# A layer of adaptive norm, long convolution and low-rank product: tables on ScalarE's queue, six weight buffers, rows in pairs

## Chip, cores and metric

The kernel runs on one core of a Trainium2 chip. The metric is the device time of one execution in microseconds. Before the change three runs took 2176.75, 2179.15 and 2181.75 us; the median is 2179.15.

## What is computed

x has 4 batches of 1024 rows of 2048 numbers, all fp32. From a short vector c per batch the modulation makes six vectors of 2048 (sections 0 to 5, in this order):

```python
mod = (silu(c) @ wmod).reshape(4, 6, 1, -1)       # wmod: 2048 x 12288
sa, ca, ga, sb, cb, gb = (mod[:, i] for i in range(6))
ga, gb = (sign(g) * max(abs(g), 0.25) for g in (ga, gb))
h = layernorm(x) * (1 + ca) + sa
x = x + ga * (causal_conv(h, K) + D * h)          # along each row, 2048 taps
h = layernorm(x) * (1 + cb) + sb
out = x + gb * (h @ W.T + bias + low_rank(h))     # 16 adapters of rank 16
```

The impulse response K comes from a state space model of 64 complex states: sums over the states at 2048 frequencies (with the parameters Lambda, p, q, Ct, Vc, Bp and log_step, and tables of cosines and sines), and an inverse Fourier transform.

## The kernel before

The work stands in stages that overlap. A tile scheduler puts each engine's instructions in a fixed order from the order of the source, the dependencies and marked priorities; each engine then takes its own list strictly in turn, and waits at a semaphore where data or a buffer is missing. The DMA queues of SP, ScalarE (ACT) and GpSimd (POOL) are lists of the same kind. Transfers share eight semaphores for SP and ACT together, taken in rotation, so that a transfer can also wait for the one that last used its semaphore.

**Modulation.** A section is 16 rows of weights (`mod_load`, L306): each a tile wm of 128 x 2048 fp32, 1 MB, loaded by SP (L309). `mod_mm` (L312) then issues four matmuls of 512 columns side by side into one PSUM tile, modps, of which there is one buffer; the left operand sct is silu(c). `section` in `net` (L792) runs over the 16 rows. At its end ScalarE copies modps to mrow (L325), TensorE transposes it (mtp, L328) and VectorE writes the column (L332): ca from section 1, sa from section 0, then both are scaled (`fold_scale`, L361 to L373). All sections share the pool wmp of WM = 3 buffers.

**Impulse response.** `toeplitz` (L233) calls `s4` (L76) with high priority. `s4` loads parameters and tables with 16 transfers of GpSimd (L86 to L107), five of them twice, for the upper and the lower 64 partitions. VectorE makes 2/step from log_step (z, L112 to L124), coefficients (L130 to L147), and in four chunks of 512 frequencies the terms of the sums: TensorE spreads the tables (s4cs, L161), VectorE and ScalarE work on wi, wr and nu (L165 to L173), TensorE sums over the states (s4rp, L176). VectorE continues on s4R (L181 to L226), TensorE ends the transform (s4kp, L229). The result kk is scaled with a maximum over partitions by GpSimd, stored to DRAM (kd, L254) and read back as overlapping rows kb (L258), all on ACT's queue. The second half of `toeplitz`, taken after row KT = 6 of section 0, reverses kb's rows on TensorE (kbps, L262) and splits it into fp16 parts kh and kl (L278 to L283).

**The start** (`net`, L838): section 1, then the loads of x blocks 0 to 2 and the statistics of blocks 0 and 1 (`conv_load`, `stats` L494), then section 0.

**Phase 1** runs over 32 blocks of 128 rows. `conv_prep` normalizes a block (n, L511), transposes it (tp, L532), modulates it (t, L535) and splits it into fp16 parts hc and hs (L541 to L544); `conv_mm` (L564) is the convolution, 108 matmuls a block; `conv_post` stores x (x1d) and the transposed second norm (n2d, L622). The gate's section 2 runs beside blocks 0 and 1. From block R0 = 3 on a filler `rest` is stepped by the plan of each block: it alternates between `merges` (low-rank product added to W, L440 lps, and operands wcd stored, L469) and the rows of sections 4, 3 and 5, one row after every MR = 2 merge steps.

**Phase 2** multiplies by the merged weights in Winograd's form (`ffn_unit`, L701), in 16 units for each half of the columns.

Of the kernel before, what the change touches and what calls it, by code (L numbers as in the profile page):

```python
# [14 lines left out]
BF16 = mybir.dt.bfloat16  # L15
# [5 lines left out]
PSUM = bass.MemoryType.PSUM  # L21
# [3 lines left out]
P = 128  # L25
D = 2048          # length of a row: model width and sequence of the convolution
NB = 4            # batches
NC = D // P       # chunks of 128 in a row
HC = NC // 2
NU = 16           # units of 256 rows  # L30
LNMAX = 46.0      # no entry of a layer norm over 2048 exceeds sqrt(2047)
FP_TOP = 4096.0   # fp16 operands are scaled to at most twice this


class Net:
# [11 lines left out]
    # ---- scales: powers of two that bring the largest entry into [top, 2*top)  # L47
# [15 lines left out]
    # ---- 1/sqrt(var + eps)  # L63
    def rstd(self, pool, var, out, n, name, scale=1.0):
        # a step of Heron's method refines the root
        v = self.nc.vector
        ve = pool.tile([P, n], F32, tag=name + "_v", name=name + "_v")
        t = pool.tile([P, n], F32, tag=name + "_t", name=name + "_t")
        v.tensor_scalar(ve, var, 0.25 * scale, 0.25e-5, MUL, ADD)
        self.nc.scalar.activation(t, ve, AF.Sqrt)  # L70
        v.reciprocal(out, t)
        v.scalar_tensor_tensor(t, ve, out, t, MUL, ADD)
        v.reciprocal(out, t)

    # ---- impulse response of the state space model: PSUM [l1, l2], l = 16*l1 + l2
    def s4(self, pool):  # L76
# [9 lines left out]
        for h in range(2):  # L86
            hp = slice(64 * h, 64 * h + 64)
            nc.gpsimd.dma_start(out=vec[hp, 0, :], in_=io["Lambda_ri"])
            nc.gpsimd.dma_start(out=vec[hp, 1, :], in_=io["p_ri"])
            nc.gpsimd.dma_start(out=vec[hp, 2, :], in_=io["q_ri"])  # L90
            nc.gpsimd.dma_start(out=vec[hp, 3, :], in_=io["Ct_ri"].rearrange("o n c -> (o n) c"))
            nc.gpsimd.dma_start(out=vc[hp], in_=io["Vc_ri"])
        bp = T([P, 64], "s4bp")
        nc.gpsimd.dma_start(out=bp, in_=io["Bp"].rearrange("m o -> (m o)").partition_broadcast(P))
        ls = T([P, 1], "s4ls")
        nc.gpsimd.dma_start(out=ls, in_=io["log_step"].partition_broadcast(P))
        # cosines and sines in three bfloat16 parts, summed and broadcast by the tensor engine
        cs = T([3, 2, D], "s4cs", BF16)
        nc.gpsimd.dma_start(out=cs, in_=io["t_cs"])
# [3 lines left out]
        nc.gpsimd.dma_start(out=csk, in_=io["t_csk"])  # L103
        tw = T([P, 2, 16, 16], "s4tw")
        nc.gpsimd.dma_start(out=tw, in_=io["t_tw"])
        dft = T([P, 2, P], "s4dft")
        nc.gpsimd.dma_start(out=dft, in_=io["t_dft"])  # L107

        # 2/step = 2*exp(-log_step): range reduction, polynomial, exponent bits
# [16 lines left out]
        # B = Vc Bp  # L126
# [5 lines left out]
        # numerators conj(ct)B, conj(ct)p, conj(q)B, conj(q)p  # L132
# [15 lines left out]
        # 1/w, w = i (2/step) S - lambda C: real part in the first 64 rows, imaginary part below  # L148
# [67 lines left out]
        # inverse transform: over k2 with the table, over k1 on the tensor engine  # L216
# [15 lines left out]
    # ---- Toeplitz operand kb[s, j] = K[j - s], in two fp16 parts; D is added to K[0]  # L232
    def toeplitz(self, pool):  # L233
# [21 lines left out]
        # row s starts P - 1 - s earlier; the tensor engine puts the rows in the opposite order  # L255
# [8 lines left out]
        # for outputs in pairs of chunks: K at even chunks (for sums of two operands), and the  # L264
        # differences to the chunk before and after; two fp16 parts each
# [21 lines left out]
    # ---- silu(c), transposed: [k = 16 p + j, batch], the batches repeated over 32 columns  # L287
# [14 lines left out]
    # ---- one section of the modulation: PSUM rows 32 q + b hold columns 512 q ..  # L302
# [18 lines left out]
    def mod_column(self, pool, name, plus_one):  # L321
        """[d in chunk, chunk, batch] of the section in modps"""
        nc, v = self.nc, self.nc.vector
        row = pool.tile([P, 512], F32, tag="mg0", name="mrow")
        nc.scalar.copy(row, self.modps)  # L325
        ps = self.tps.tile([P, 4, P], F32, tag="t", name="mtp")
        for c in range(4):
            nc.tensor.transpose(ps[:, c, :], row[:, ds(P * c, P)], self.ident)  # L328
        col = self.const(name, [P, NC, NB])
        src = ps.rearrange("p c (q r) -> p q c r", r=32)[:, :, :, 0:NB]  # L330
        dst = col.rearrange("p (q c) b -> p q c b", c=4)
        v.tensor_scalar(dst, src, plus_one, None, ADD)  # L332
        return col

    def mod_gate(self, pool, name, bias=None):
        """the gate by rows, in DRAM; with bias also gate*bias"""
        nc, v = self.nc, self.nc.vector
        g = pool.tile([P, 512], F32, tag="mg0", name="mg0")
        v.tensor_copy(g, self.modps)
        m = pool.tile([P, 512], F32, tag="mg1", name="mg1")  # L340
        nc.scalar.activation(m, g, AF.Abs)
        v.tensor_scalar(m, m, 0.25, None, ALU.max)
        v.tensor_scalar(g, g, 0.0, 2.0, ALU.is_ge, MUL)
        v.scalar_tensor_tensor(g, g, 1.0, m, SUB, MUL)
        outs = [g]
        if bias is not None:
            bt = pool.tile([P, 512], F32, tag="mg2", name="mg2")
            for q in range(4):
                nc.sync.dma_start(out=bt[32 * q : 32 * q + 32], in_=bias[ds(512 * q, 512)].partition_broadcast(32))
            v.tensor_tensor(bt, bt, g, MUL)  # L350
            outs.append(bt)
        res = []
        for i, t in enumerate(outs):
            dr = self.dram.tile([NB, D], F32, tag=f"{name}{i}", name=f"{name}{i}")
            for q in range(4):
                nc.scalar.dma_start(out=dr[:, ds(512 * q, 512)], in_=t[32 * q : 32 * q + NB])
            res.append(dr)
        return g, res

    # ---- scales of the normalized, modulated rows, per batch; folded into the columns in place  # L360
# [15 lines left out]
    # ---- low-rank factors in two fp16 parts; w_e and the inverse scale of A go into B  # L376
    def prep_lora(self, pool, tmp):
# [9 lines left out]
        # no entry exceeds the norm of its row  # L387
# [32 lines left out]
    # ---- merged weights of d chunks c and c + 8; the seven right operands in DRAM  # L420
    def merge(self, pool, tmp, c):
# [22 lines left out]
        # no entry exceeds the norm of its row  # L444
# [44 lines left out]
    # ---- phase 1: layer norm, modulation, transposed operand of the convolution  # L489
# [29 lines left out]
    def conv_prep(self, pl, r, x, st, out):  # L519
# [4 lines left out]
        # fp16 parts of the chunks, and of the sums of an even chunk and the odd one after it  # L524
# [70 lines left out]
    def conv_late(self, x, y, sums):  # L595
        """gate and residual of a block whose convolution ran before the gate was there"""
        v = self.nc.vector
        for q in range(2):
            sl = ds(1024 * q, 1024)
            v.tensor_tensor(y[:, sl], y[:, sl], self.gat[:, sl], MUL)  # L600
            v.scalar_tensor_tensor(y[:, sl], y[:, sl], 1.0, x[:, sl], MUL, ADD, accum_out=sums[:, q : q + 1])

    # ---- the second layer norm, transposed
# [21 lines left out]
    def gate_tile(self, pool, b):  # L625
        """the gate of a batch with the scales of the convolution's operands taken off, in all rows"""
# [14 lines left out]
    # ---- phase 2: left operands of the seven products of a unit  # L641
# [48 lines left out]
    def ffn_unit(self, pl, u, q, lf, wc):  # L690
# [34 lines left out]
        # Winograd's form; P4 comes with the opposite sign  # L725
# [28 lines left out]
M0, MR = 0, 2  # L754
# [3 lines left out]
WM = 3  # L758
LEFT0 = 30
KT = 6  # L760
# [11 lines left out]
def net(ctx: ExitStack, tc: tile.TileContext, io):  # L772
# [19 lines left out]
    def section(sec):  # L792
        for q in range(16):
            if q == 0:
                k.mod_begin()
            k.mod_mm(k.mod_load(wmp, sec, q), q)
            yield
# [32 lines left out]
    toe = k.toeplitz(pool(st, "st", 1))  # L830
    with tc.high_priority():
        take(toe, 1)
# [3 lines left out]
    for sec in (1, 0):  # L836
        for i, _ in enumerate(section(sec)):
            take(mer, M0)  # L838
            if sec == 0 and i == KT:
                with tc.issue_after(k.last.ins):  # L840
                    take(toe, 1)
        if sec == 1:
            for r in range(3):
                xs[r] = k.conv_load(pl, r)
            for r in range(2):
                sts[r] = k.stats(pl, xs[r], "1")
    st.close()
    for name, bufs in (("h", 2), ("n", 2), ("t", 2), ("y", 2), ("g", 1), ("nt", 2)):
        pl[name] = pool(left, "p1" + name, bufs)
    def rest():  # L850
        mods = (x for sec in (4, 3, 5) for x in section(sec))
# [18 lines left out]
    def load_w(q, i):  # L870
        """the two halves of a right operand; two of them take the places of x"""
# [29 lines left out]
    sec = section(2)  # L901
# [3 lines left out]
    take(sec, 16)  # L905
# [76 lines left out]
def tables():  # L982
    """cosines and sines; they depend on the shapes alone"""
# [17 lines left out]
def layout(inputs):  # L1001
# [4 lines left out]
    # [chunk pair, row of the pair's operand, half of e, half of d, d]  # L1006
# [20 lines left out]
```

## Time and profile before

| what | us |
|---|---|
| median of three runs | 2179.15 |
| the profiled execution, first to last instruction | 2174.4 |
| what lies between that span and the median | 4.75 |
| TensorE busy | 2090.6 |
| VectorE busy | 1356.8 |
| ScalarE busy | 938.0 |
| first matmul of section 1 | 6.5 |
| first matmul of section 0 | 72.75 |
| last matmul of section 0 ends | 121.3 |
| mean clock granted to TensorE, share of full | 0.975 |

The profiled execution has no separate time of its own: its span of 2174.4 us is read beside the median of the runs. A line of a timeline gives start, duration, engine, source line, operation, what is written and read, count, and in brackets the engine's idle time ahead of it with what ended it. PE is TensorE, PEld its weight loads, DVE VectorE, ACT ScalarE, POOL GpSimd; a q behind a name is that engine's queue. A line of the windows gives the stretch, its length, the busy time and instruction count of PE, PEld, DVE, ACT and POOL, then TensorE's clock, the DMA engines' busy share and GB/s.

### The profile page before, as it was taken

The numbers are of one execution on the slowest core, as the hardware profiler recorded it, in microseconds if no ns is written. First come the engines' busy times: TensorE is split into PE (matmuls) and PEld (weight loads), VectorE is DVE, ScalarE is ACT, GpSimd is POOL, SyncE is SP. The second block draws the span as 40 slices with busy tenths as digits, with TensorE's granted clock in tenths as the row PEclk, the third lists the DMA queues.
The fourth block names the chain that finished last, engine by engine and source line by source line (L and its number), as shares of the span: only waits on it lengthen the run. The fifth ranks groups of instructions, "written<-read, shape, count | busy, mean of one in ns | idle before, by whom it ended". The sixth has DMA issues, their size and how long they took to land.

```text
span 2174.4 us, 28541 instructions
## 1 busy us (share of the span) xinstructions
PE 2090.6 (96%) x11084; PEld 1020.7 (47%) x11084; DVE 1356.8 (62%) x2293; ACT 938.0 (43%) x1795; POOL 11.7 (1%) x28
## 2 busy tenths in 40 slices
PE   4699999999999999999999999999999999999998
PEld 1234555555555555565444444444444444444443
DVE  5637898888989999974666666666533333333333
ACT  0046877767867778863353545454300000000000
POOL 1000000000000000000000000000000000000000
PEclk6589999999999999999999999999999999999999
DMA  7988687888788656747766666666785544544541
GB/s 273 368 325 307 232 315 271 300 313 299 278 307 300 219 204 232 257 136 294 264 223 232 222 219 221 232 223 225 285 332 192 174 164 164 175 165 165 172 157 68
DMA packets 207307, 516.62 MB, mean 238 GB/s; under 512 B 16112, under 2 KB 81665, under 8 KB 180289
## 3 DMA queue, kind: packets, MB, share of 16 engines
q1 hardware_dynamic: 206208, 513.11, 66.3%
q8 instruction: 87, 1.43, 0.3%
q10 hardware_dynamic: 388, 1.16, 0.1%
q0 software_dynamic: 576, 0.54, 0.1%
q14 instruction: 48, 0.39, 0.1%
HBM read 325.89 MB, written 188.85 MB: 237 GB/s over the span
## 4 chain that ended last, share of the span: by engine, by line
PE 64%; DVE 13%; ACT 8%; DMA 6%; issue 2%; SPq 1%; DVEq 0%; ACTq 0%
PE fZ L701 18%; PE fY L701 12%; PE fX L701 11%; PE ya L564 9%; PE yb L564 5%; PE lps L440 3%; PE modps L314 3%; DMA gt<-n2d 2%; DVE lf L662 2%; ACT gt L651 2%; PE tp L620 2%; DVE s L668 1%; ACT t L535 1%; ACT n L611 1%; PE tp L532 1%
## 5 line engine op out<-in xcount | busy, mean ns | idle before, releaser
L701 PEld LDWEIGHTS <-lf 128*128 128x128 f16 x5376 | 526.4, 98 | 642.0 <-issue 10.2
L701 PE MATMUL fZ<-w,lf 128*128 128x512 f16 x2304 | 514.8, 380 | 6.2 <-ACT p L709 6.1
L701 PE MATMUL fX<-w,lf 128*128 128x512 f16 x1536 | 342.6, 379 | 0.0
L701 PE MATMUL fY<-w,lf 128*128 128x512 f16 x1536 | 342.5, 379 | 0.0
L564 PEld LDWEIGHTS <-hc 128*128 128x128 f16 x2304 | 215.7, 98 | 187.9 <-issue 31.9
L717 DVE TENSOR_TENSOR xo<-xo,gb 128x1024 f32<-128x1024 f32 x64 | 78.3, 1224 | 204.6 <-DMA xo<-x1d 204.5
L535 ACT ACTIVATE t<-tp,sa,ca 128x128 f32<-128x128 f32 x512 | 200.1, 471 | 6.0 <-DVE sa L373 3.8
L651 ACT ACTIVATE gt<-gt,sb,cb 128x256 f32<-128x256 f32 x256 | 132.1, 594 | 148.2 <-DMA gt<-n2d 147.4
L564 PE MATMUL ya<-kh,hs 128*128 128x512 f16 (+3 forms) x768 | 192.9, 326 | 0.9 <-ACT hs L543 0.9
L564 PE MATMUL ya<-kh,hc 128*128 128x512 f16 (+3 forms) x768 | 192.7, 326 | 0.5 <-ACT qs L577 0.5
L564 PE MATMUL yb<-kh,hc 128*128 128x512 f16 (+3 forms) x768 | 192.5, 326 | 0.0
L314 PE MATMUL modps<-wm,sct 128*32 128x512 f32 x768 | 132.1, 728 | 27.9 <-DMA wm<-in_wmod 27.9
L564 PEld LDWEIGHTS <-hs 128*128 128x128 f16 x1152 | 107.5, 98 | 96.9 <-issue 15.9
L709 ACT COPY p<-fZ 128x512 f32<-128x512 f32 x64 | 37.3, 583 | 256.9 <-PE fZ L701 256.9
L709 ACT COPY p<-fX 128x512 f32<-128x512 f32 x32 | 18.5, 578 | 268.7 <-PE fX L701 255.7
L564 PE MATMUL ya<-kl,hc 128*128 128x512 f16 (+3 forms) x384 | 125.1, 326 | 0.0
L564 PE MATMUL ya<-kl,hs 128*128 128x512 f16 (+3 forms) x384 | 125.1, 326 | 0.0
L564 PE MATMUL yb<-kl,hc 128*128 128x512 f16 (+3 forms) x384 | 125.1, 326 | 0.0
L661 ACT CAST lf<-s 128x1024 f16<-128x1024 f32 x64 | 67.2, 1050 | 102.5 <-DVE s L668 75.8
L621 ACT COPY nt<-tp 128x512 f32<-128x512 f32 x128 | 74.8, 597 | 60.0 <-PE tp L620 40.9
L544 DVE TENSOR_TENSOR hc<-t,hc 128x512 f16<-128x512 f32 x128 | 87.3, 682 | 6.3 <-ACT hc L543 5.8
L723 DVE TENSOR_TENSOR xo<-xo,fin 128x512 f32<-128x512 f32 x128 | 88.2, 689 | 3.1
(247 smaller groups left out, 2234.3 us busy)
## 6 DMA issues: line engine op xcount, KB each, us to landing
wm<-in_wmod SPq DMA_DIRECT2D x96, 1024.0 KB
lfd<-lf SPq DMA_DIRECT2D x112, 512.0 KB
lf<-lfd SPq DMA_DIRECT2D x112, 512.0 KB
x<-in_x SPq DMA_DIRECT2D x32, 1024.0 KB
x1d<-y SPq DMA_DIRECT2D x32, 1024.0 KB
n2d<-nt SPq DMA_DIRECT2D x128, 256.0 KB
gt<-n2d SPq DMA_DIRECT2D x128, 256.0 KB
xo<-x1d SPq DMA_DIRECT2D x64, 512.0 KB
```

What stands on the lines that cost most here:

```text
L314: self.last = self.nc.tensor.matmul(self.modps[32 * g : 32 * g + 32, :], self.sct[:, j].rearrange("p r b -> p (r b)"), w[:, ds(512 * g, 512)],
L440: nc.tensor.matmul(ps, la[:, x, k, h], y[:, k, osl], start=(n == 0), stop=(n == 5))
L535: nc.scalar.activation(t[:, k], tp[:, k], AF.Identity, bias=self.sa[:, c, b : b + 1], scale=self.ca[:, c, b : b + 1],)
L544: v.tensor_tensor(lo[:, sl], src, hi[:, sl], SUB)
L564: nc.tensor.matmul(pf[:, o:512], h, self.kf[f][z][:, ds(k0, 512 - o)], start=first, stop=(i == last and (x, z) == (1, 0)), skip_group_chec ...
L621: nc.scalar.copy(nt, tp)
L651: nc.scalar.activation(t[:, c], t[:, c], AF.Identity, bias=self.sb[:, c, b : b + 1], scale=self.cb[:, c, b : b + 1],)
L661: nc.scalar.copy(hl[:, :, 0, :], s)
L701: nc.tensor.matmul(ps[name], lf[i][:, k, x, :], wc[i][k // 4][:, k % 4, y, :], start=(first and n == 0), stop=(n == 3 * HC - 1), skip_grou ...
L709: nc.scalar.copy(t, ps[name])
L717: v.tensor_tensor(x, x, self.gbias, ADD)
L723: v.tensor_tensor(xs[r][:, h], xs[r][:, h], t, ADD)
```

## The change

Three things change; comments in the source go too, which moves line numbers only.

```diff
 # s4: loads of parameters and tables
-        for h in range(2):
-            hp = slice(64 * h, 64 * h + 64)
-            nc.gpsimd.dma_start(out=vec[hp, 0, :], in_=io["Lambda_ri"])
...
-            nc.gpsimd.dma_start(out=vc[hp], in_=io["Vc_ri"])
+        def twice(x, n):
+            return bass.AP(tensor=x.tensor, offset=x.offset, ap=[[0, 2], [n, 64], [1, n]])
+        ls = T([P, 1], "s4ls")
+        nc.scalar.dma_start(out=ls, in_=io["log_step"].partition_broadcast(P))
+        nc.scalar.dma_start(out=vec[:, 0, :], in_=twice(io["Lambda_ri"], 2))
+        cs = T([3, 2, D], "s4cs", BF16)
+        nc.scalar.dma_start(out=cs, in_=io["t_cs"])
+        nc.scalar.dma_start(out=vc, in_=twice(io["Vc_ri"], 128))
         bp = T([P, 64], "s4bp")
-        nc.gpsimd.dma_start(out=bp, in_=io["Bp"].rearrange("m o -> (m o)").partition_broadcast(P))
...
+        nc.scalar.dma_start(out=bp, in_=io["Bp"].rearrange("m o -> (m o)").partition_broadcast(P))
+        for i, n in ((1, "p_ri"), (2, "q_ri"), (3, "Ct_ri")):
+            nc.scalar.dma_start(out=vec[:, i, :], in_=twice(io[n], 2))
...
-        nc.gpsimd.dma_start(out=csk, in_=io["t_csk"])
+        nc.scalar.dma_start(out=csk, in_=io["t_csk"])
...
 # net
-M0, MR = 0, 2
+MR = 4
-WM = 3
+WM, WMS = 3, 3
+X0 = (7, 11)
-KT = 6
+KT = 8
...
-    def section(sec):
-        for q in range(16):
-            if q == 0:
-                k.mod_begin()
-            k.mod_mm(k.mod_load(wmp, sec, q), q)
+    def section(sec, n, pools):
+        k.mod_begin()
+        for q in range(0, 16, n):
+            ws = [k.mod_load(pools[j % len(pools)], sec, j) for j in range(q, q + n)]
+            for j, w in enumerate(ws):
+                k.mod_mm(w, q + j)
             yield
...
+    wms = pool(st, "wms", WMS)
...
     for sec in (1, 0):
-        for i, _ in enumerate(section(sec)):
-            take(mer, M0)
+        for i, _ in enumerate(section(sec, 1, (wms, wmp))):
             if sec == 0 and i == KT:
                 with tc.issue_after(k.last.ins):
                     take(toe, 1)
-        if sec == 1:
-            for r in range(3):
+            if sec == 0 and i in X0:
+                r = X0.index(i)
                 xs[r] = k.conv_load(pl, r)
-            for r in range(2):
                 sts[r] = k.stats(pl, xs[r], "1")
+    xs[2] = k.conv_load(pl, 2)
     st.close()
...
-        mods = (x for sec in (4, 3, 5) for x in section(sec))
+        mods = (x for sec in (4, 3, 5) for x in section(sec, 2, (wmp,)))
...
-    sec = section(2)
+    sec = section(2, 2, (wmp,))
...
-    take(sec, 16)
+    take(sec, 8)
```

The 16 transfers of GpSimd become 11 on ACT's queue, in a new order: log_step, Lambda, the cosine table, Vc, Bp, then p, q and Ct, the table csk, tw and dft; those that were made twice now read their source twice with a step of 0. Sections 1 and 0 take their rows alternately from wms and wmp, six buffers together; wms lies in the stack `st`, which is closed after section 0, and the pools of phase 1 take its place. Blocks 0 and 1 of x are loaded after rows 7 and 11 of section 0, block 2 after its last row. Sections 2, 4, 3 and 5 load two rows and then issue both rows' matmuls; the filler takes such a pair after every four merge steps. In the built order of TensorE, the first five s4cs matmuls now stand ahead of section 1's first row.

More of the change, by code (lines that the diff above doesn't have):

```diff
@@ L85, in s4 @@
         vc = T([P, 64, 2], "s4vc")
-        for h in range(2):
-            hp = slice(64 * h, 64 * h + 64)
[L88 to L91, printed above, removed]
-            nc.gpsimd.dma_start(out=vc[hp], in_=io["Vc_ri"])
-        bp = T([P, 64], "s4bp")
-        nc.gpsimd.dma_start(out=bp, in_=io["Bp"].rearrange("m o -> (m o)").partition_broadcast(P))
[L95 to L99, printed above, removed]
+        def twice(x, n):
[6 more added lines that the diff above has]
+        nc.scalar.dma_start(out=vc, in_=twice(io["Vc_ri"], 128))
+        bp = T([P, 64], "s4bp")
+        nc.scalar.dma_start(out=bp, in_=io["Bp"].rearrange("m o -> (m o)").partition_broadcast(P))
+        for i, n in ((1, "p_ri"), (2, "q_ri"), (3, "Ct_ri")):
+            nc.scalar.dma_start(out=vec[:, i, :], in_=twice(io[n], 2))
         one = T([3, P], "s4one", BF16)
@@ L102, in s4 @@
         csk = T([P, 2, 16], "s4csk")
-        nc.gpsimd.dma_start(out=csk, in_=io["t_csk"])
+        nc.scalar.dma_start(out=csk, in_=io["t_csk"])
         tw = T([P, 2, 16, 16], "s4tw")
-        nc.gpsimd.dma_start(out=tw, in_=io["t_tw"])
+        nc.scalar.dma_start(out=tw, in_=io["t_tw"])
         dft = T([P, 2, P], "s4dft")
-        nc.gpsimd.dma_start(out=dft, in_=io["t_dft"])
+        nc.scalar.dma_start(out=dft, in_=io["t_dft"])
         z = T([P, 4], "s4z")
```

## Prediction

> **What bounds the kernel now.** I read the page's busy line and slices first, then the timelines of TensorE, GpSimd and ScalarE over the first 125 us, then the windows and waits.
>
> ```profile
> PE 2090.6 (96%) x11084; PEld 1020.7 (47%) x11084; DVE 1356.8 (62%) x2293; ACT 938.0 (43%) x1795; POOL 11.7 (1%) x28
> PE   4699999999999999999999999999999999999998
> PEclk6589999999999999999999999999999999999999
> ```
>
> TensorE bounds it from the third slice (54 us each) on. In the first two it is 40 and 60% busy at a clock of 0.5 to 0.6. So the prize lies in the first 121 us: the two modulation sections, 32 rows of 1 MB.
>
> ```profile
> 18.55 1.93 PE L314 MATMUL modps<-wm,sct 128*32 128x512 f32 x8 [0.64 <-DMA wm<-in_wmod]
> 29.84 2.29 PE L161 MATMUL s4cs<-s4cs,s4one 3*128 3x512 bf16 x5 [9.35 <-DMA s4cs<-in_t_cs]
> ...
> 61.10 1.88 PE L176 MATMUL s4rp<-s4coef,s4nu 128*128 128x8 f32 x8 [1.43 <-DVE s4nu L173]
> 62.90 3.64 PE L314 MATMUL modps<-wm,sct 128*32 128x512 f32 x16
> ...
> 72.75 1.93 PE L314 MATMUL modps<-wm,sct 128*32 128x512 f32 x8 [1.91 <-DMA wm<-in_wmod]
> 75.16 1.94 PE L314 MATMUL modps<-wm,sct 128*32 128x512 f32 x8 [0.47 <-DMA wm<-in_wmod]
> ...
> 119.34 1.93 PE L314 MATMUL modps<-wm,sct 128*32 128x512 f32 x8 [0.56 <-DMA wm<-in_wmod]
> ```
>
> TensorE stands 9.35 us for the cosine table, then takes rows two at a time between steps of VectorE's chain. A row costs 1.85 us at this clock (3.64 for two); rows arrive 2.48 us apart when transfers run freely (75.16 - 72.75 and the next). With three buffers the transfers stop whenever TensorE does:
>
> ```profile
> 20.00:30.00 10.00, 0.65 (x5) 0.20 (x2) 3.33 (x29) 0.00 (x0) 3.42 (x7) 0.50 0.74 245
> 30.00:66.00 36.00, 28.35 (x128) 9.98 (x126) 33.53 (x70) 4.82 (x8) 0.00 (x0) 0.55 0.77 282
> 66.00:72.70 6.70, 2.70 (x12) 1.65 (x8) 5.55 (x18) 1.87 (x2) 0.00 (x0) 0.50 1.00 419
> ```
>
> The last columns are clock, DMA share and GB/s: 245 and 282 against 419. Why the table is late:
>
> ```profile
> 1.25 0.85 POOL L88 DMA_DIRECT2D s4vec<-in_Lambda_ri  x1 [0.32 <-issue]
> 13.60 0.28 POOL L237 TENSOR_SCALAR_AFFINE_SELECT rev<-rev 128x128 f32<-128x128 f32 x1 [11.50 <-issue]
> ...
> 21.77 0.57 POOL L99 DMA_DIRECT2D s4cs<-in_t_cs  x1
> ```
>
> The reader is to see that the table is not slow to move but late to be asked for: GpSimd stands 11.5 us ahead of its mask, then issues a transfer each 0.55 us, and the cosine table is the thirteenth; it lands 8.0 us after issue (the page's list of issues).
>
> **Part 1, tables by ACT's queue.** Removed: 16 GpSimd transfers and that delay. Added: 11 issues on ScalarE at 0.23 to 0.53 us (its two early ones). The mask still waits to 13.6, but its first users now (identity: section 1's transpose, past 55) hide that; were they the first matmuls, it would cost 11 us. In the built order a transfer waits for the one that last used its semaphore: rows 2 and 3 on SP wait for the cosine table and Bp, p for log_step, Ct for Lambda, csk for row 0 (landed at 6.5), and ScalarE's tanh is queued behind csk. VectorE's sct follows that tanh among the products with Ct, so row 0's matmul starts near 12.5, not 6.51. That is hidden: six rows can be on their way, the last landing at 4 + 6 x 2.5 = 19, and row 6's buffer is free at 14.4; with three buffers it would stop the transfers from 11.5 on. Landing after issue: 2.1 us on empty queues (mc, issued 0.72, used 2.85) to 4.9 us under load (kd<-kk, 77.99 to 82.95).
>
> Two rules of the Trainium skill speak against this part, both in "DMA: Bandwidth & Descriptors". By "Issuing engines are not separate DMA queues", changing the issuer saves only issue time: by it 16 x 0.55 less 11 x 0.4, an estimated 4 us. The trace decides: the 11.5 us stand before the issues, the queues are not the limit. "Rules for kernel authors" says that a leading zero-stride broadcast of c copies keeps a transfer on c engines; the doubled loads have c = 2. Five of the eleven are confined so, which no run here shows; I price it at nothing to 5 us on Ct, taking 2, since they are small. So Ct lands at about 10 (7 to 14): issue 5, landing 3, confinement 2.
>
> The chain then, by VectorE's rows of before: coefficients, tanh products and sct 3.5, to 13.5; first combine (33.62) to s4R (63.01) 29.4, to 43; s4R to the last sum 6.3 without the column step, and its matmul 0.8, to 50. kk to its scaled form took 7.1 us, of which some 5 were statistics of x, now later: 2, to 52. Kd, then kb: 5.0, to 57. In the new order section 1's mrow stands on ScalarE behind both issues:
>
> ```profile
> 66.61 0.59 ACT L325 COPY mrow<-modps 128x512 f32<-128x512 f32 x1 [10.55 <-PE modps L314]
> ...
> 77.99 0.35 ACTq L254 DMA_DIRECT2D kd<-kk  x1
> 82.95 0.35 ACTq L258 DMA_DIRECT2D kb<-kd  x1
> ```
>
> Queued behind mrow are the square roots; waiting for it are the transpose and, since modps has one buffer, all of section 0. Rows 13 to 15 follow kp and end at 50 + 3 x 1.85 = 55.6, so the new wait costs 1.4 us. mrow 0.6 and transpose 1.1: row 16 starts at 58.7, where before it was 72.75.
>
> **Part 2, six buffers and later x.** Without stops, 32 rows, two x, kb and 0.5 MB of tables are 35.5 x 2.5 = 89 us from about 4: 93. Stops left: row 22 needs row 16's buffer (60.5), by when kb and row 21 are still moving (to 62); I take 2 us. TensorE: 58.7 + 16 x 1.85 + kbps 6.6 = 95 without a pause; I take 97 with row waits, the page's code fetches and the first bytes. Before, the last row ended at 121.3: gain 24.3. The kbps block, which cost a stop of 5 us (99.6 to 105.5), is now bridged by buffers. Extra space costs no work. The pools opened after st.close() wait for row 30, two rows ahead of their first use: nothing, 2 us if they are late.
>
> x0 lands before row 24, x1 before row 28, x2 after row 31. x2's four statistics (0.62 each) now stand among the steps that scale ca and sa; three lie on the path to the first activation: 1.9 us lost. Section 2's first row comes behind x2, 5 us after row 31, while TensorE needs 4.5 us to reach it: 0.5 at most, within my rounding. The kb splits and x1's normalization end near 97.5, beside the sa step; hidden, but if kbps slips, they slip on.
>
> **Part 3, row pairs, MR 4.** The 64 row and merge matmuls move, none is added. A pair holds TensorE 2.0 us instead of 1.0 twice. The fill gets shorter: in the built order the last merge product stands at convolution matmul 2052, formerly 2376, the first at 360 in both: 15.7 blocks of 108 instead of 18.7. Is VectorE the bound then? It is busy for 445 of 500 us (windows, 300 to 800), 0.89, that is 25.4 us of a block's 28.5. Its merge steps are 131 of 450 us (groups, 250 to 700), 8.3 a block; times 18.7 / 15.7 they are 9.9, so 27.0. TensorE's share, 48 rows of 1.0 and 384 products of 0.216 (twelve took 2.59), 131 us, goes from 7.0 to 8.3 a block, 29.8 in all. 27.0 / 29.8 = 0.91: not yet. SP is the other risk (waits of SP, then of whom, us, times, longest; 200 to 1010):
>
> ```profile
> SPq L622 <- ACT nt L621: 288.0, 83, 17.9
> SPq L309 <- PE modps L314: 78.0, 17, 14.6
> ```
>
> SP stands 78 us behind row buffers already; behind such a load stand the stores of n2d, x1d and wcd and the loads of x. Yet TensorE's own waits there are some 20 us in all, none for a row. No trace shows pairs: between 3 us won (fewer changes of work) and 10 lost (half as many waits again); I take 1.4 lost, near the row for single ones, since the built order loads a pair's rows well ahead of its matmuls.
>
> Sum: 24.3 - 1.9 - 1.4 = 21. The span 2174.4 becomes 2153.4; the profiled times stand 4.75 below the median 2179.15 (work around the span), so 2158.
>
> **Rivals.** (a) Larger, 12%: no stop and TensorE at a higher clock (a run of three rows took 2.78 us at 99.62); section 0 ends at 93, 2179 - 27 = 2152. (b) Smaller, 20%: the doubled loads land late (Ct at 20), all behind them shifts by 10 us, mrow too, and section 0 ends at 107: 2168. For it: the semaphore chain through row 0 and ScalarE's order; against: ACT's queue is empty and the loads are under 64 KB. (c) It does not do what it says, 5%: the early gain is lost again where VectorE is near its limit (780 to 930, where it is 91 to 100% busy and TensorE 93%); some 2 us remain: 2177. (d) Slower, 8%: the pair's second load holds SP till the pair before has passed TensorE, stores of wcd behind it stop ScalarE's and VectorE's two-buffer steps, and TensorE's transposes wait. Price: 24 pairs at 1.1 us = 26, against a gain of 24.3 - 1.9 = 22.4: 2183. It decides from 0.93 us a pair. For it: n2d's 288 us of waits show how much SP stands; against: no matmul of modps waited after 200 us.
>
> **How the numbers follow.** My case, 55%, spans 2153 to 2165. With most of (a) and (b), 2148 to 2172 leaves two in ten out. Faster: 0.55 + 0.12 + 0.20 = 0.87; within 0.2% (4.4 us, about what this measurement can tell from no change): (c), 0.05; slower: (d), 0.08.
>
> **What would show it.** Right: s4cs before 8 us, section 0's first row near 59, its last near 97 (121), DMA above 350 GB/s from 20 to 95, convolutions about 22 us earlier throughout, TensorE's waits in the fill still near 20 us. Wrong: VectorE waiting past 12 us for s4vec, mrow after 62, rows of section 0 waiting for landings, or waits of tp and modps after 200 us grown by over 10 us.

## The result and the profile after

The changed kernel takes 2184.77 us (median of 13 runs, 2180.71 to 2190.86) beside 2179.15 us for the one before (13 runs, 2176.75 to 2184.43). The ratio is 1.0024, with an interval of 1.0015 to 1.0034: some 5 us slower. The forecast was 2158 and its range ended at 2172.

The profiled execution of after has a span of 2185.9 us and a time of its own of 2187.76, 3 us above its median. In all later executions the time is 1.7 to 2.1 us longer than the span (1.86 here), so the profiled one of before took some 2176.3, 3 us below its median. The spans therefore show 11.5 us where the medians show 5.6. Sizes are taken below from ratios and medians, places from the traces; a difference of few us between the later parts of two traces is not read.

The page's busy line and slices of after:

```profile
PE 2084.6 (95%) x11084; PEld 1026.0 (47%) x11084; DVE 1355.3 (62%) x2293; ACT 939.6 (43%) x1795; POOL 2.7 (0%) x12
...
PE   4699999999999999999999999999999999999998
...
PEclk8689999999999999999999999999999999999999
```

TensorE's slices tell the two kernels apart only by the clock of the first two (8 and 6 tenths, where 6 and 5 stood). The start has to be read row by row. TensorE's timeline of after:

```profile
13.02 2.29 PE L162 MATMUL s4cs<-s4cs,s4one 3*128 3x512 bf16 x5 [13.02 <-DVE s4zi L123]
23.87 5.33 PE L315 MATMUL modps<-wm,sct 128*32 128x512 f32 x24 [8.57 <-DVE s4t L142]
...
61.62 0.61 PE L230 MATMUL s4kp<-s4zz,s4dft 128*128 128x16 f32 x2 [0.97 <-DVE s4zz L227]
...
70.44 1.08 PE L329 MATMUL mtp<-ident,mrow 128*128 128x128 f32 x4 [3.33 <-ACT mrow L326]
71.45 5.45 PE L315 MATMUL modps<-wm,sct 128*32 128x512 f32 x40
...
110.50 1.93 PE L315 MATMUL modps<-wm,sct 128*32 128x512 f32 x8 [0.56 <-DMA wm<-in_wmod]
```

The first matmul runs at 13.02, where before row 0 ran at 6.51; row 0 now starts at 23.87. Section 0 starts at 71.45, only 1.3 us earlier than before, and ends at 112.4 instead of 121.3. The head start is 8.9 us, not 24.3. ACT's queue shows what was issued when:

```profile
1.22 1.12 ACTq L92 DMA_DIRECT2D s4vec<-in_Lambda_ri  x1
2.37 0.29 ACTq L95 DMA_DIRECT2D s4cs<-in_t_cs  x1
...
3.26 6.28 ACTq L98 DMA_DIRECT2D s4bp<-in_Bp  x1
...
12.92 1.27 ACTq L100 DMA_DIRECT2D s4vec<-in_Ct_ri  x1
```

VectorE's first use of Lambda and of Ct:

```profile
12.79 0.17 DVE L151 TENSOR_SCALAR s4nl<-s4vec 128x2 f32<-128x2 f32 x1 [7.88 <-DMA s4vec<-in_Lambda_ri]
...
22.39 0.16 DVE L140 TENSOR_TENSOR s4t<-s4vec,s4bq 128x1 f32<-128x1 f32 x1 [5.03 <-DMA s4vec<-in_Ct_ri]
```

Lambda, 1 KB, was issued at 1.22, and VectorE could use it only at 12.8, after 11.6 us. The cosine table was issued early and came just behind, at 13.0. Bp's issue took 6.28 us of the queue, and Ct was issued at 12.92 and used at 22.4. The waits of SP's queue from 0 to 115 us (who waited for what: us in total, times, longest) show the damage:

```profile
SPq L310 <- PE modps L315: 52.9, 21, 6.8
...
SPq L310 <- DMA s4cs<-in_t_cs: 10.8, 1, 10.8
SPq L310 <- DMA s4vec<-in_Ct_ri: 7.5, 1, 7.5
```

The loads of rows 2 and 4 stood for the cosine table and for Ct, 18.3 us together, because they take over the semaphores of those transfers. So four of the six buffers stood empty until 13.0 (row 2's load was issued at 12.99). In the windows from 10 to 15 us of after and then of before, the last column is GB/s:

```profile
10.00:15.00 5.00, 1.98 (x5) 0.54 (x4) 1.94 (x12) 0.00 (x0) 0.54 (x2) 1.00 0.54 63
```

```profile
10.00:15.00 5.00, 1.65 (x14) 0.16 (x8) 0.00 (x0) 0.00 (x0) 1.39 (x3) 0.86 0.99 333
```

The second loss lies in the fill. The last merge product ends at 716.8 us instead of 774.4, as the built order said, but between 300 and 700 us TensorE is busy for 9.7 us less (before, then after; the first busy time is PE's, the third VectorE's):

```profile
300.00:700.00 400.00, 395.88 (x2512) 214.53 (x2510) 352.55 (x680) 285.53 (x578) 0.00 (x0) 1.00 0.86 301
```

```profile
300.00:700.00 400.00, 386.19 (x2427) 209.68 (x2425) 347.17 (x664) 282.77 (x555) 0.00 (x0) 1.00 0.87 309
```

VectorE is not busier than before, so its busy share does not explain this. TensorE's longest group of waits from 250 to 1000 us is for ScalarE's t, ahead of the transposes; before and after:

```profile
PE tp L532 <- ACT t L535: 5.4, 8, 1.4
```

```profile
PE tp L533 <- ACT t L536: 13.4, 13, 1.7
```

A third loss lies between the two. Block 3 of the convolution took 47.8 us, where before it took 37.6. Some of that is filler moved into it; but TensorE stood idle for 6.7 us in it instead of 2.3, at a lower clock (block 3 of after, then of before; the third figure from the end is the clock):

```profile
208.80:256.60 47.80, 41.15 (x220) 20.94 (x221) 36.64 (x78) 34.94 (x70) 0.40 (x1) 0.93 0.74 263
```

```profile
216.20:253.80 37.60, 35.28 (x201) 19.59 (x202) 33.00 (x69) 30.86 (x62) 0.40 (x1) 0.95 0.78 274
```

### The profile page after: what moved, and what is told of

The parts are those of the page before. It is cut to its first block, busy times and chain, and to the rows that moved or that the text cites. A ratio compares the mean times of both kernels' runs of the same rounds, so it can differ in the third digit from the quotient of the medians.

```text
span 2185.9 us, 28516 instructions
## 1 busy us (share of the span) xinstructions
PE 2084.6 (95%) x11084; PEld 1026.0 (47%) x11084; DVE 1355.3 (62%) x2293; ACT 939.6 (43%) x1795; POOL 2.7 (0%) x12
## 4 chain that ended last, share of the span: by engine, by line
PE 55%; issue 24%; DVE 10%; DMA 6%; ACT 5%; SPq 1%; ACTq 1%; POOL 0%; DVEq 0%; POOLq 0%
PE fZ L702 20%; PE fY L702 13%; PE fX L702 13%; PE ya L565 4%; PE yb L565 2%; DVE lf L663 2%; DMA gt<-n2d 2%; ACT t L536 1%; DMA wm<-in_wmod 1%; DVE s L669 1%; PE modps L315 1%; ACT gt L652 1%; DMA xo<-x1d 1%; ACT n L612 1%; PE tp L621 1%
## 5 line engine op out<-in xcount | busy, mean ns | idle before, releaser
L565 PEld LDWEIGHTS <-hs 128*128 128x128 f16 x1152 | 108.0, 98 | 92.7 <-issue 12.7
L315 PE MATMUL modps<-wm,sct 128*32 128x512 f32 x768 | 122.3, 693 | 28.7 <-DMA wm<-in_wmod 20.1
L533 PE MATMUL tp<-ident,n 128*128 128x128 f32 x512 | 80.5, 282 | 18.0 <-ACT t L536 16.0
L495 DVE BATCH_NORM_STATS2 st<-x 128x6 f32<-128x512 f32 x128 | 83.0, 680 | 18.4 <-DMA x<-in_x 18.4
```

Of the source, the lines that this page charges most:

```text
L315: self.last = self.nc.tensor.matmul(self.modps[32 * g : 32 * g + 32, :], self.sct[:, j].rearrange("p r b -> p (r b)"), w[:, ds(512 * g, 512)],
L495: v.bn_stats(st[:, q], x[:, ds(512 * q, 512)])
L533: nc.tensor.transpose(tp[:, k], n[:, ds(P * (c0 + k), P)], self.ident)
L565: nc.tensor.matmul(pf[:, o:512], h, self.kf[f][z][:, ds(k0, 512 - o)], start=first, stop=(i == last and (x, z) == (1, 0)), skip_group_chec ...
```

## The experiments

Two questions followed. Why did the tables land late, and what does each part of the change cost by itself? The first four kernels take them up. They ran beside a median of 2182.44 us for before (55 runs).

**Tables alone.** The kernel before with the 11 transfers of ACT's queue, three buffers and single rows.

```diff
-            nc.gpsimd.dma_start(out=vec[hp, 0, :], in_=io["Lambda_ri"])
+        nc.scalar.dma_start(out=vec[:, 0, :], in_=twice(io["Lambda_ri"], 2))
...
```

> The kernel before with the 11 table transfers on ScalarE's queue, nothing else. In the profile of after, Lambda landed at 12.8 us and the last of Ct near 16.8, the response's last matmul (s4kp) ended at 62.2 instead of 70.8, and TensorE stood 8.6 us for sct. Theory (doubled loads confined to few engines are late, but still earlier than GpSimd's): s4kp about 8 us earlier, with three buffers a part of it is lost again; section 0 ends 3 to 8 us earlier, 2171 to 2176. Rival (the new place on ScalarE's queue is itself the harm: sct and mrow stand behind transfers): section 0 ends no earlier, 2179 to 2184.

Measured 2180.45, ratio 0.9987 (0.9978 to 0.9996): 1 to 5 us gained. Section 0 ended at 118.6, 2.7 us earlier, a little under the theory's 3 to 8. The start is as late as in after: Lambda used at 12.7, row 0 at 20.2. The tables come earlier than from GpSimd, but the first rows pay for it.

**Buffers alone.** GpSimd's tables, single rows, six buffers, x after rows 7 and 11 and after row 15, the second half of `toeplitz` after row 8.

```diff
-        for i, _ in enumerate(section(sec)):
+        for i, _ in enumerate(section(sec, 1, (wms, wmp))):
```

> The kernel before with six buffers for sections 1 and 0, x loaded after rows 7, 11 and 15 of section 0 and KT 8; tables stay on GpSimd, later rows single. Theory: the buffers bridge TensorE's standing for the tables and the kbps block (some 5 us), x2's late statistics cost 2: section 0 ends 4 to 10 us earlier, 2170 to 2177, and nothing is lost in the blocks from 3 on. Rival (the new start, with x2's statistics and pools that wait for wms, disturbs the blocks that follow): block 31 at least 8 us later than section 0's end would give, 2180 to 2190.

Measured 2179.38, ratio 0.9979 (0.9971 to 0.9988). Section 0 ended at 112.5, as early as in the whole change, with the tables as late as before: the buffers alone give 8.8 us. Some 4.6 of them reach the end (2.6 to 6.3 by the interval).

**Pairs alone.** The start of before, sections 2 to 5 by pairs.

```diff
-MR = 2
+MR = 4
...
-        mods = (x for sec in (4, 3, 5) for x in section(sec))
+        mods = (x for sec in (4, 3, 5) for x in section(sec, 2, (wmp,)))
```

> The kernel before with later sections by row pairs and a pair after every four merge steps, nothing else. In the profile of after, block 3 stood 4 us ahead of before and block 31 10 us behind. Theory (the loss of some 15 us is made by the pairs and the denser fill): start as before, block 31 later by 10 to 18 us, 2189 to 2197. Rival (the loss comes out of the changed start): 2177 to 2182.

Measured 2195.10, ratio 1.0049 (1.0032 to 1.0065): 7 to 14 us lost, where the prediction had 1.4. This part alone turns the change from a gain into a loss.

**Halved loads.** The whole change, but each doubled load is two loads of 64 partitions, on the same queue; 16 transfers in place of 11.

```diff
-        def twice(x, n):
...
+        def both(out, x):
+            for h in range(2):
+                nc.scalar.dma_start(out=out[64 * h : 64 * h + 64], in_=x)
...
-        nc.scalar.dma_start(out=vec[:, 0, :], in_=twice(io["Lambda_ri"], 2))
+        both(vec[:, 0, :], io["Lambda_ri"])
...
```

> The changed kernel with each of the five doubled loads split in two loads of 64 partitions, still on ScalarE's queue, so 16 transfers; the leading step of 0 is gone. Theory (confinement to few engines makes Lambda, the cosine table behind it and Ct late): Lambda lands by 6 us, SP's row 2 goes out by 7 instead of 12.9, sct by 16 instead of 23, section 0 ends 5 to 10 us earlier than 112.4, 2174 to 2180. Rival (lateness comes from the semaphores in rotation and ScalarE's order, which more transfers make worse): section 0 ends at 112 or later, 2184 to 2188.

Measured 2181.48, ratio 0.9997 (0.9988 to 1.0007), with the pairs still in it: some 6 us faster than the whole change by the ratios, whose intervals lie apart. TensorE's timeline, VectorE's first use of Lambda and one window:

```profile
15.71 4.74 PE L315 MATMUL modps<-wm,sct 128*32 128x512 f32 x24
...
101.40 1.94 PE L315 MATMUL modps<-wm,sct 128*32 128x512 f32 x8 [0.56 <-DMA wm<-in_wmod]
```

```profile
9.89 0.17 DVE L151 TENSOR_SCALAR s4nl<-s4vec 128x2 f32<-128x2 f32 x1 [4.93 <-DMA s4vec<-in_Lambda_ri]
```

```profile
10.00:15.00 5.00, 2.29 (x5) 0.67 (x5) 4.32 (x18) 1.54 (x2) 0.54 (x2) 1.00 0.91 307
```

Row 0 starts 8.2 us earlier than in after, section 0 ends at 103.3 instead of 112.4, and the DMA engines move 307 GB/s where they moved 63. So the form of the loads, with what hangs on it, was the fault. The theory was too hopeful in two places: Lambda was used at 9.9 instead of 6, and row 2's load went out at 9.81 instead of 7. By the Trainium skill ("DMA: Bandwidth & Descriptors", "Rules for kernel authors") a leading broadcast of two copies holds a transfer to at most two of the sixteen engines, and the recovery agrees with that. So do the trace's records of single DMA packets: the first 128 packets of 8 bytes on ACT's queue, Lambda's by size and order, moved from 6.0 to 12.1 us in after and from 5.2 to 9.0 here, though issued at the same time beside the same two rows. The edit also shifts which semaphore each load takes over, and SP still stood 7.6 us for Lambda; so beyond these 3 us the run does not say how much of the 8.2 is due to either.

The next four ask whether gains and costs add, and what it is about pairs that costs. They ran beside a median of before of 2182.30 us (27 runs).

**The change without its pairs.**

```diff
-MR = 4
+MR = 2
...
-        mods = (x for sec in (4, 3, 5) for x in section(sec, 2, (wmp,)))
+        mods = (x for sec in (4, 3, 5) for x in section(sec, 1, (wmp,)))
```

> The change without its pairs: MR 2 and single rows in sections 2 to 5, the tables on ACT's queue and six buffers kept. Theory (the pairs cost some 13 us by themselves, as in before with pairs alone, and costs and gains add): the whole change stands some 2 to 6 us above before, so this stands 7 to 11 us below it, ratio 0.995 to 0.997; convolution block 31 begins some 10 us earlier than in the whole change. Rival (a head start is taken back in the fill whatever the rows do): within 4 us of before, ratio 0.998 to 1.000, like six buffers alone.

Measured 2173.56, ratio 0.9963 (0.9949 to 0.9978). The theory holds: the first two parts gain 5 to 11 us, the third gives more than that back. Section 0, which this edit does not touch, ended at 109.0 instead of 112.4: single traces of the same start differ by some 3 us there.

**Without pairs, loads halved.** Both edits together.

> As the run before, and each doubled load is issued as two loads of 64 partitions. Theory (gains add): section 0 ends near 103 us as in the halved loads with pairs, 18 us ahead of before, and without the pairs' cost the time is some 13 us below before, ratio 0.993 to 0.995. Rival (the head start is taken back in blocks 3 and 4 and 8 to 14): 3 to 5 us below, ratio 0.998.

Measured 2170.06, ratio 0.9950 (0.9935 to 0.9965). Section 0 ended at 106.2, convolution block 1 began 12.9 us earlier than before, and by ratio and medians 11 to 12 us of that reach the end (8 to 14 by the interval). The rival's 3 to 5 us fall. The part due to the halving is not separated from the run before by these intervals.

**Pairs at the old pace.** Pairs alone again, but the filler rests a step after each pair, so that the fill is as long as before.

```diff
                 next(mods, None)
                 yield
+                yield
```

> Before with pairs alone, but the filler rests for one step after each pair, so that merge steps and rows come at the pace of before and the fill is as long as in before. Theory (the loss comes from the shorter, denser fill: VectorE's and ScalarE's steps of a block are crowded by more merge steps): the loss goes, within 3 us of before, ratio 0.9985 to 1.0015. Rival (the loss comes from taking two rows together, which holds TensorE or the queue longer at a time): still 9 to 14 us above before, ratio 1.004 to 1.0065.

Measured 2185.98, ratio 1.0019 (1.0012 to 1.0025): some 4 us lost, just outside the theory's band.

**Single rows at the pairs' pace.** The kernel before, but the filler hands back control only after every second row.

```diff
                 next(mods, None)
-                yield
+                if n % 4 == 0:
+                    yield
```

> Before with single rows, but the filler hands back control only after every second row, so that the fill has the pace of the pairs' one and ends as early. Theory (density): as slow as before with pairs alone, 9 to 14 us above before, ratio 1.004 to 1.0065; the last merge product stands near 720 us. Rival (pairing): within 3 us of before, ratio 0.9985 to 1.0015.

Measured 2191.67, ratio 1.0045 (1.0033 to 1.0058), some 9 us lost without a single pair; the last merge product ended at 721.6. So some 4 us (3 to 5) belong to taking two rows together and 9 (7 to 13) to the pace; their sum, 13, is about what pairs alone cost (11 by the ratio, 13 by the medians). Windows of pairs alone, of single rows at that pace and of pairs at the old pace:

```profile
300.00:700.00 400.00, 386.79 (x2429) 209.17 (x2427) 347.07 (x665) 286.36 (x562) 0.00 (x0) 1.00 0.87 309
```

```profile
300.00:700.00 400.00, 390.51 (x2434) 207.59 (x2433) 351.16 (x666) 286.01 (x563) 0.00 (x0) 1.00 0.85 303
```

```profile
300.00:700.00 400.00, 389.00 (x2468) 214.35 (x2467) 347.50 (x674) 281.57 (x571) 0.00 (x0) 1.00 0.82 293
```

TensorE idles 13 and 9 us in the first two, against 4 before, and no engine is busier by more than 1 us. The waits are many short ones, up to about 2 us, more than half of them for ScalarE's t. But pairs at the old pace idle 11 us there too, and cost only 4: this window shows the kind of loss, and the split into 4 and 9 rests on the times alone.

The next three start from the best kernel so far (halved loads, single rows) and ran beside a median of before of 2179.53 us (22 runs).

**A longer fill.** One resting step after every second row.

```diff
                 next(mods, None)
                 yield
+                if n % 4 == 0:
+                    yield
```

> The best so far (tables on ACT's queue with halved loads, six buffers, single rows: 0.995 of before), with one more resting step of the filler after every second row, so that the fill of merges and rows ends some three blocks later (last merge product in block 25 instead of 22). Theory (the denser the fill, the more TensorE waits for ScalarE's and VectorE's steps; 3 blocks shorter cost 9 us): 3 blocks longer wins something, less than 9 since TensorE waits only some 8 us more in those blocks than in the free ones; ratio 0.992 to 0.994. Rival (at the old pace the crowd is gone, and what TensorE waits there has other reasons): ratio 0.9945 to 0.9965.

Measured 2167.59, ratio 0.9946 (0.9932 to 0.9960): nothing gained beyond its starting point. A shorter fill costs, a longer one does not pay.

**A still longer fill.** The resting step after every row.

> As the run before with the resting step after every row: the last merge product in block 28. Theory: again a little faster, 0.991 to 0.994. Rival: no gain (0.994 to 0.997), or a loss, since the merged weights' stores and the first weights of phase 2 come late, against the end of phase 1: above 0.997.

Measured 2184.61, ratio 1.0022 (1.0014 to 1.0029). The last merge product ended at 901.2, and the start of phase 2 came late. TensorE's waits from 850 to 1050 us:

```profile
PE fX L702 <- ACT lf L662: 10.6, 1, 10.6
```

**The response's transfers by GpSimd.** kd (both writes) and kb are issued by GpSimd, so that mrow on ScalarE does not stand behind them.

```diff
-        nc.scalar.dma_start(out=kb, in_=src)
+        nc.gpsimd.dma_start(out=kb, in_=src)
```

> The best so far, with the three transfers of the impulse response (zeros and kk to DRAM, the overlapping rows back) issued by GpSimd instead of ScalarE, so that section 1's mrow on ScalarE no longer stands behind them. Theory of the prediction (section 0's start is set by mrow behind kd and kb): mrow comes some 6 us earlier, at 59 to 60 us, row 16 at 61, and section 0 ends 4 to 6 us earlier; ratio 0.992 to 0.9935. Rival (section 0 ends when its last rows have landed, whenever it begins): row 16 at 61 but the last row within 2 us of 106, ratio 0.9945 to 0.9955.

Measured 2163.39, ratio 0.9928 (0.9914 to 0.9941). TensorE's timeline:

```profile
61.85 0.63 PE L329 MATMUL mtp<-ident,mrow 128*128 128x128 f32 x4 [0.81 <-ACT mrow L326]
62.41 4.50 PE L315 MATMUL modps<-wm,sct 128*32 128x512 f32 x40
...
101.15 1.94 PE L315 MATMUL modps<-wm,sct 128*32 128x512 f32 x8 [0.58 <-DMA wm<-in_wmod]
```

Row 16 starts at 62.4, 5.1 us earlier than with halved loads and single rows alone, but the section's end moves 3.1 us (106.2 to 103.1), and the longest fill, without this edit, had it at 102.0. From the sixth row on every row waits for its landing, except the three behind the kbps block. So mrow sets the start of section 0 and the transfers its end. The two ratios' intervals overlap, so a gain from this edit is likely but not shown.

**The filler one block later.** In every kernel with six buffers so far, block 3 took some 5 to 9 us more, beyond what its matmuls need at full clock, than in before (an estimate from the pace of the same matmuls elsewhere in the traces). In the trace of the run above, ScalarE's timeline has the low-rank factors' steps in one piece there, 7.6 us ahead of the next hc and t:

```profile
217.35 3.90 ACT L415 ACTIVATE lb<-lb,lsb_s 128x2048 f32<-128x2048 f32 x2
221.15 3.68 ACT L416 CAST lbh<-lb 128x2048 f16<-128x2048 f32 x2
```

```diff
-R0 = 3
+R0 = 4
```

> The fastest so far (0.9928 of before: tables on ACT's queue with halved loads, six buffers, single rows, the three transfers of the impulse response by GpSimd) with the filler begun at block 4 instead of 3; in the built order ScalarE's four steps of lb and lbh, which stood together there, are then spread among the others. Theory (with six buffers TensorE loses 5 to 7 us at blocks 3 and 4, because these 7.6 us stand in one piece on ScalarE ahead of t): TensorE's idle time from block 1 to block 5 falls from 16 to 11 us, and the time by some 5, ratio 0.9895 to 0.9915. Rival (the crowd moves one block on, or is regained by waits later): idle unchanged by block 8 and ratio 0.992 to 0.9945.

Measured 2155.82 beside 2182.84 (5 and 9 runs), ratio 0.9878 (0.9857 to 0.9900): 22 to 31 us faster than before, the fastest kernel of this study. The same steps then stand apart:

```profile
221.39 2.00 ACT L415 ACTIVATE lb<-lb,lsb_s 128x2048 f32<-128x2048 f32 x1 [0.54 <-DVE lsb_s L55]
224.24 1.91 ACT L416 CAST lbh<-lb 128x2048 f16<-128x2048 f32 x1
229.98 2.03 ACT L415 ACTIVATE lb<-lb,lsb_s 128x2048 f32<-128x2048 f32 x1
232.69 1.93 ACT L416 CAST lbh<-lb 128x2048 f16<-128x2048 f32 x1
```

Block 4 began 25.1 us after block 3 instead of 45.2; 8.7 of these 20.1 us are matmul work moved on. From block 1 to block 5 TensorE stood idle for 1.6 us instead of 8.5, at a mean clock of 1.00 instead of 0.97, and the convolutions ended 12.1 us earlier, of which 1.7 stood already at block 1. By the ratios the step is some 11 us, about twice the one expected. A window over the 25.1 us of block 3 in this run, and ahead of it the same stretch of the run above, where block 3 began 1.7 us later, shows why:

```profile
197.70:222.80 25.10, 17.86 (x100) 8.69 (x95) 21.98 (x56) 23.33 (x48) 1.03 (x1) 0.86 0.94 334
```

```profile
197.70:222.80 25.10, 24.75 (x160) 14.96 (x161) 24.51 (x61) 24.47 (x59) 0.59 (x1) 1.00 0.85 295
```

Where TensorE stood, it was idle for 7.2 us and its granted clock fell to 0.86; where it did not, the clock stayed at 1.00. So the waits came with slower matmuls and cost twice: behind the mean of 0.86 stand two stretches of 3.4 us at 0.5 in the trace's clock records, which makes up to 3.4 us beside the 7.2. That the waits lowered the clock is read from this pair of traces; and the edit moves the whole filler by a block, so the share of lb's four steps alone is not shown.

## Why the prediction was wrong

Two terms of the sum failed, and a third was missing. Predicted was 21 us of gain, measured 5.6 of loss: 26.6 us apart by the medians. The end of section 0 was 15.4 us later than predicted (112.4 against 97), and pairs cost 11 to 13 where 1.4 stood, some 11 more. By the medians these two make up the miss. By the spans it is 32.5 us (2185.9 against 2153.4), and most of the 6 left over is block 3 (4 us more idle, and a lower clock), for which the sum had no term.

- **Landing of the doubled loads** ("I price it at nothing to 5 us on Ct, taking 2, since they are small"; "Ct lands at about 10"). Ct was used at 22.4, beyond my bound of 14. Lambda's 1 KB took 11.6 us beside two rows of 1 MB, ACT's queue stood in Bp's issue, and all landed late in turn. From sct to the end of the transform I had 36.5 us (13.5 to 50) and 38.4 were measured (23.8 to 62.2); from row 16 to the section's end 38.3 and 41.0. So the rows of VectorE's chain were read rightly and were only started 10 us late; the section's end lost some 5 more on the way. Rival (b), at 20%, had this mechanism with Ct at 20; it ended section 0 at 107.
- **"That is hidden: six rows can be on their way."** I had seen in the built order that rows 2 and 3 wait for the cosine table and Bp, and treated a late row 0 as harmless. With the table late, the rows' loads stood 10.8 and 7.5 us, and buffers that nobody fills hide nothing.
- **mrow behind both issues.** The order was read rightly: mrow stood behind kb (69.3) and came at 69.7, costing 3.3 us at the transpose instead of 1.4. But it matters less than I thought, since the landings set the end.
- **Later x.** I counted 1.9 us and up to 0.5 more. Block 1 now begins 43.4 us after section 0's last row instead of 40.6: 2.8. The size was right; its division is not tested.
- **Pairs, the term of 1.4.** The prediction asked whether VectorE becomes the bound, found 0.91 and stopped. That was true and no answer: VectorE was not the bound, and the time grew by some 9 us with the pace alone; the trace shows waits of up to 2 us on ScalarE and VectorE in turn. The shorter fill, noted as a fact, was the larger part of the cost.
- **Rival (d)** ended on the right side by another way. SP's waits for row buffers from 200 to 1010 us fell from 78.0 to 32.6, and its price, 11 to 13 us over 24 pairs, is about 0.5 us a pair, under the 0.93 from which it was to decide. It decided because the gain that it had to beat was 6 us (8.9 - 2.8), not 22.4. What in the denser fill makes each wait is not settled: SP's stores of wcd stood longer for VectorE (114.0 us against 69.7), and this went with the pace (115.0 for single rows at the pairs' pace, 67.3 for pairs at the old one); but no run took that alone away.
- **Rival (c)** falls by the times: with single rows, convolution block 1 began 9.9 and 12.9 us early, and 8 to 9 and 11 to 12 us of that show in the medians and ratios. The traces show less: the convolutions of these two ended at 995.1 and 994.6, before's at 996.2. Their executions stood 2 and 7 us above their medians and before's below its own, so this does not size the gain; but the greater part of the head start that these traces lose goes at block 3 (202 to 252 us), not where (c) looked for it (780 to 930).
- **Of the signs listed**, DMA above 350 GB/s from 20 to 95 us came (375), and with it the six buffers' gain; s4cs before 8, row 16 near 59, the end near 97 and waits near 20 us in the fill (33) did not. Of the signs of being wrong, Lambda past 12 us, mrow past 62 and rows waiting for landings came; the waits of tp and modps after 200 us grew by 8, not by over 10.

## What to carry to other kernels

Before small loads are moved to another queue, ask three things of each: over how many engines its access pattern spreads, what large transfers move beside it, and which later transfer takes over its semaphore; a late small load can then stop the large ones. An engine's busy share under 1 does not make a denser stage free: price the pace itself, by a run that changes only the number of steps. And look for long single steps on an engine that others wait for in short turns: starting the filler one block later, which set them apart, brought about as much as the whole earlier start.

## What the runs showed that was not expected

Pauses in the middle of the kernel can come with a lower clock of TensorE: 7 us of waits in block 3 came with 0.86, and 0.85 in the change without its pairs over the whole block (205 to 252 us); with the waits gone it was 1.00. Not all do: 5.7 us of waits between 750 and 800 us, in single rows at the pairs' pace, left it at 1.00. A 1 KB load of two 64-partition copies took 11.6 us to be usable beside two rows of 1 MB, and a 32 KB load's issue occupied ScalarE's queue for 6.28 us; with the copies as separate loads Lambda was used at 9.9 instead of 12.8, and Bp's issue took 0.61 us, with the queue standing 2.8 us ahead of the next load. The fill has an optimum of pace that is flat on one side: 3 blocks shorter cost some 9 us (from the kernel before), 3 blocks longer nothing, 6 blocks longer 17 us more by the medians (both from halved loads with single rows), of which the trace shows 13 as waits at the start of phase 2.
